# x turned by transfers and one VectorE block transpose instead of by TensorE transposes

## The chip, the cores and the metric

The kernel runs on one core of a Trainium2 chip. TensorE (PE in the profile) multiplies matrices into PSUM; VectorE (DVE), ScalarE (ACT) and GpSimd (POOL) do elementwise work; SyncE (SP) issues the DMAs, all on one queue and in program order. Each engine takes its own instructions in program order and waits for the others through semaphores. The metric is the device time of one execution in microseconds.

## The reference, cut to what matters

x has shape 8 x 2048 x 512: 16384 tokens of 512 features. Two sublayers follow each other. In the attention the axes are named so that, for every token, its 16 heads of 32 numbers attend to each other. The second sublayer routes tokens to experts with a capacity of 8 // 16 = 0, so no expert takes a token, and it comes down to norms:

```python
h = layernorm(x)
Q, K, V = h @ Wq.T + bq, h @ Wk.T + bk, h @ Wv.T + bv     # (8, 2048, 512) -> (8, 16 heads, 2048, 32)
scores = einsum('nqhd,nkhd->nhqk', Q, K) / sqrt(32)       # q, k: heads; h: token
out = einsum('nhql,nlhd->nqhd', softmax(scores), V)       # (8, 16, 2048, 32), read as (8, 2048, 512)
x = x + layernorm(out.reshape(8, 2048, 512) @ Wo.T + bo)
y = layernorm(layernorm(x)) * ln_g + ln_b                 # what is left of the second sublayer
x = x + layernorm(y)
```

All of it is in float32. The products take their left and right operands with the summed index on the partitions, so x, which arrives with tokens on the partitions, has to be turned once so that features lie there.

## The kernel before, in words

The 16384 tokens are 32 units of 512 tokens. A unit is four tiles of 128 tokens; tile t belongs to unit t // 4. Work is written out by hand as strings of two-letter items, and the order of these strings is the program order on every engine at once.

**One tile of x.** `load_x` (L239) brings it into one of four buffers `x`. `stat_x` (L252) takes mean and variance on DVE (L183, L184) and the inverse deviation on POOL (L190, L191). `norm_x` (L257) normalises in place on DVE (L260) and sets the last column to 1 on POOL (L261), because that row of the turned x carries the bias. `turn_x` (L263) makes four 128x128 transposes on TensorE into a PSUM bank `px` (L267), which comes from the same pool of four banks (tag `pj`) as some products. `keep_x` (L270) copies the bank into `xb` on ACT: tiles 0 and 1 of a unit whole (L279), tiles 2 and 3 only their second half (L281). `add_x` (L283) forms four sums of quarters for tiles 2 and 3: two on DVE that read PSUM (L290, L291) and two on POOL (L292, L293). `xb` has seven slots of 2 x 256 columns.

**The products.** Each of q, k and v is a 512x512 by 512x512 product, made with seven products of quarters (`multiply`, L300) instead of eight. Products 1, 6, 7 and 4 of one matrix add up, one on top of the other, in the same PSUM bank ("a"); after each of them `collect` (L323, items `q1e`, `q6e`, ...) copies what the bank then holds on ACT. So 6 can begin only when `1e` has read the bank, 7 only after `6e`, and 4 only after `7e`. Products 5 and 3 share a second bank in the same way: 3 waits for `5e`, which is on DVE. The right operands of products 1 to 7 are slots of `xb`; product 6 needs a sum that POOL makes. The output projection (`d1` to `d7`, `out_multiply` L496 and `out_collect` L512) has the same form: `d6e` and `d7e` are ACT copies at L516, `d5e` is on DVE, and `d6` needs POOL's sums `oS` (`sB`, L476 to L480).

**Steps.** Unit u is worked through in four steps (`step`, L712; strings `STEPS`, L692, and `FIRST_STEPS`, L703, for unit 0). In step c, softmax and weighing of quarter c of unit u run beside the products of unit u+1 (q in steps 0 and 1, k in 1 and 2, v in 2 and 3), the output projection of unit u (d1 in step 3) and of u-1 (the rest in step 0), the final norms of rows of unit u-1 (ra, rv, rg, rf, rt, re, rs), and the reading in of x for unit u+2 (xs, xn, px, xa, xt). The softmax chain of a step is `mx` (DVE maximum and difference, ACT exponential), `dn` (DVE sum and reciprocal, POOL product), `tr` (DVE block transpose, L426), `x0` to `x3` (four ACT copies, L431). Every step ends on TensorE with `sc` (scores, L393) and `av` (weighing, L442); the next step begins with `ok`, the ACT copy of the weighed values, and `mx`.

q, k and v go through DRAM to be spread over partitions: `write` (L356: qs, ks, vs) and `spread_qk`, `spread_v` (L369, L378: qd, kx, vd), four DMAs per matrix and direction. `sk` (kx) is at the head of step 3 and must land before that step's `sc`.

`first_unit` (L597) prepares tiles 0 to 7 and makes the products of unit 0; `last_unit` (L781) ends with the norms of the last rows.

Of the kernel before, what the change touches and what calls it, by code (L numbers as in the profile page):

```python
# [34 lines left out]
F32 = mybir.dt.float32  # L35
BF16 = mybir.dt.bfloat16
AF = mybir.ActivationFunctionType
ALU = mybir.AluOpType
# [12 lines left out]
def head_attention_norms(  # L51
# [15 lines left out]
    nc = tc.nc  # L67
    NB, S, E = x.shape
    P = 128
    H, D = 16, 32  # L70
    assert NB // H == 0, "experts that take tokens"
    EC = E // P
    Q4 = 4
# [7 lines left out]
    xpool = ctx.enter_context(tc.tile_pool(name="xpool", bufs=4))  # L81
    pool2 = ctx.enter_context(tc.tile_pool(name="pool2", bufs=2))
# [24 lines left out]
    oS = const.tile([P, Q4, 2, 2 * P], F32, name="oS")  # L107
    junk = const.tile([P, E], F32, name="junk")
# [130 lines left out]
    def load_x(t):  # L239
        if t < NT:  # L240
            xs[t] = xpool.tile([P, E], F32, tag="x", name=f"x_{t}")
            n, s = divmod(P * t, S)
            nc.sync.dma_start(xs[t], x[n, s : s + P, :] if t < NT - Q4 else renumbered[t % Q4])
# [8 lines left out]
    def stat_x(t):  # L252
        if t < NT:
            mv = moments(xs[t], f"x{t}")
            xrs[t] = mv, rsqrt(mv[:, 1:2], f"x{t}", 1.0, EPS)

    def norm_x(t):  # L257
        if t < NT:
            mv, rs = xrs.pop(t)
            nc.vector.tensor_scalar(xs[t], xs[t], mv[:, 0:1], rs, ALU.subtract, ALU.mult)  # L260
            nc.gpsimd.memset(xs[t][:, E - 1 : E], 1.0)  # L261

    def turn_x(t):  # L263
        if t < NT:
            px[t] = ps_pj.tile([P, EC, P], F32, tag="pj", name=f"px_{t}")
            for ec in range(EC):
                nc.tensor.transpose(px[t][:, ec, :], xs[t][:, ec * P : (ec + 1) * P], ident)  # L267
            del xs[t]

    def keep_x(t):  # L270

        if t < NT:
            u, J = divmod(t, Q4)
            if J == 0:
                xb[u] = pool2.tile([P, 7, 2, 2 * P], F32, tag="xb", name=f"xb_{u}")
            j = slice(P * (J % 2), P * (J % 2) + P)
            if J < 2:
                dst = xb[u][:, 0:2].rearrange("p n e t -> p (n e) t")[:, :, j]
                nc.scalar.copy(dst, px[t])  # L279
            else:  # L280
                nc.scalar.copy(xb[u][:, 2, :, j], px[t][:, 2:4])  # L281

    def add_x(t):  # L283

        if t < NT and t % Q4 >= 2:
            u, J = divmod(t, Q4)
            j = slice(P * (J % 2), P * (J % 2) + P)
            b11, b21, b22, t1, t2, t3, t4 = (xb[u][:, n, :, j] for n in range(7))
            b12 = px[t][:, 0:2]
            nc.vector.tensor_tensor(t3, b22, b12, ALU.subtract)  # L290
            nc.vector.tensor_tensor(t1, b12, b11, ALU.subtract)  # L291
            nc.gpsimd.tensor_tensor(t2, b22, t1, ALU.subtract)  # L292
            nc.gpsimd.tensor_tensor(t4, b21, t2, ALU.subtract)  # L293
# [6 lines left out]
    def multiply(u, name, n):  # L300
        if n == 1:
            banks[name, "a"] = ps_a.tile([P, E], F32, tag="pa", name=f"pa{name}_{u}")
        elif n in (2, 5):
            banks[name, n] = ps_pj.tile([P, E], F32, tag="pj", name=f"p{name}{n}_{u}")
        ps = banks[name, {2: 2, 5: 5, 3: 5}.get(n, "a")]
        w, t = weights[name], sums[name]
        lo, hi = slice(0, 256), slice(256, 512)
        left = {
            1: w[:, 0:2, lo], 2: w[:, 2:4, lo], 3: w[:, 0:2, hi], 4: w[:, 2:4, hi],
            5: t[:, 0], 6: t[:, 1], 7: t[:, 2],  # L310
        }[n]
        right = xb[u][:, {1: 0, 2: 1, 3: 2, 4: 6, 5: 3, 6: 4, 7: 5}[n]]
        if name == "v":
            left, right = right, left
        for m in range(2):
            for e in range(2):
                nc.tensor.matmul(  # L317
                    ps[:, 256 * m : 256 * m + 256],
                    lhsT=left[:, e, P * m : P * m + P], rhs=right[:, e, :],
                    start=(n in (1, 2, 5) and m == 0 and e == 0), stop=(e == 1), skip_group_check=True,  # L320
                )
# [47 lines left out]
    def spread_qk(u, name):  # L369
        if name == "q":  # L370
            qd[u] = pool2.tile([P, H, P], F32, tag="qd", name=f"qd_{u}")
        for J in range(Q4):
            d = slice(32 * J, 32 * J + 32)
            dst = qd[u][d] if name == "q" else kx[d, J % 2]
            src = scratch[name][J // 2, :, J % 2].rearrange("g (d h) t -> d g (h t)", d=D)
            nc.sync.dma_start(dst.rearrange("d (g h) t -> d g (h t)", g=Q4), src)
# [220 lines left out]
    def first_unit():  # L597
# [14 lines left out]
        norm_x(0)  # L612
        turn_x(0)
        keep_x(0)
        stat_x(2)
        norm_x(1)
        turn_x(1)
        keep_x(1)
        stat_x(3)
        norm_x(2)  # L620
        turn_x(2)
        keep_x(2)
        norm_x(3)
        turn_x(3)
        keep_x(3)
# [6 lines left out]
        add_x(2)  # L632
        less_last("q", nc.vector, (1,))
        add_x(3)
# [22 lines left out]
        spread_qk(0, "k")  # L657
        stat_x(6)
        run(0, "v2 v2e v2w v6 v6e")
        turn_x(4)  # L660
        keep_x(4)
        norm_x(6)
        turn_x(5)
# [3 lines left out]
        keep_x(5)  # L667
        load_x(9)
        norm_x(7)
        turn_x(6)  # L670
        keep_x(6)
        load_x(10)
        add_x(6)
        turn_x(7)
        keep_x(7)
        run(0, "v5 v4 v5e v4e v4w v5w")
        stat_x(8)
        add_x(7)
# [4 lines left out]
    def run(u, items):  # L683
# [9 lines left out]
        "lx lr sv st ok sB px mx xa q1 q1e ra d2 ou dn d2e rv d6 d6e tr d5 x0 x1 x2 x3 d7 d7e rg rf q2 rt d5e xs"  # L693
        " d4 q2e re xn d4e d3 d3e rs q2w st sc av",
        "lx lr q6 q6e mx ra dn ok ou q5 rv q7 tr q7e x0 x1 x2 x3 k1 rg rf q5e k1e rt q4 xs q3 q4e re k2 q3e xn"
        " q5w q4w rs px st xa q3w k2e sc av",
        "lx lr k6 k6e mx ra dn ok ou k5 rv k7 tr k7e k2w x0 x1 x2 x3 v1 sq rg k5e rf v1e rt k4 xs k4e k5w k3 re xn"
        " k3e k4w rs px st xa xt k3w sc av",
        "sk lx lr v2 mx v2e ra v6 ok v6e dn ou ds v5 rv sA v7 tr x0 x1 v7e x2 x3 d1 rg rf v5e v2w d1e v4 rt xs"
        " v4e v5w v3 re xn v3e v4w rs px xa xt v3w sc av",  # L700
# [3 lines left out]
        "lx sv mx q1 q1e dn ok ou q2 q2e q6 q6e tr k1 k1e x0 x1 x2 x3 q7 q7e q2w lb xs q5 q5e xn q4 q4e px q5w q4w lo"  # L704
        " xa sc av",
        "lx k2 mx k2e dn ok ou c4 q3 tr k6 k6e x0 x1 x2 x3 q3e k2w q3w k5 xs cs k7 k7e c0 k5e xn px k5w xa sc av",
        "lx mx v1 v1e dn ok ou k4 k4e k3 k3e tr k4w k3w sq c1 v2 x0 x1 x2 x3 v2e xs c2 c3 v6 v6e xn wt px xa xt v2w sc av",
        "sk lx ds v7 v7e mx v5 v5e dn ok ou xs tr v4 v4e xn x0 x1 x2 x3 d1 sA v4w v5w d1e px v3 v3e xa xt v3w lg sc av",
# [3 lines left out]
    def step(u, c):  # L712
# [8 lines left out]
        def keep_last():  # L721
# [9 lines left out]
            "xs": lambda: stat_x(s + 9), "xn": lambda: norm_x(s + 9), "px": lambda: turn_x(s + 8),  # L731
# [3 lines left out]
            "xa": lambda: keep_x(s + 8), "xt": lambda: add_x(s + 8),  # L735
# [142 lines left out]
```

## Time and profile before

| What | Value |
|---|---|
| median of 3 runs | 1885.3 us (1884.98 to 1886.38) |
| span of the profiled execution | 1882.1 us, 3.2 us under that median |
| granted TensorE clock | 0.995 on the mean |
| steps of unit 15 to 16 on TensorE (905.8 to 963.2 us) | 16.0, 14.3, 12.6 and 14.5 us, together 57.4 us |
| busy in these 57.4 us | PE 57.40, DVE 43.93, ACT 36.54, POOL 31.77 us |
| DMA share in the four steps | 0.62, 0.33, 0.80, 0.83 |
| TensorE transposes of x | 512 in the whole, four per tile, 16 per unit |

The rows of the profile name the line, the engine, the operation and the tiles it writes and reads (`px<-ident,x`), with the number in the brackets at the end giving the idle time of the engine before it and what ended it. In the chain a line gives the start, the length and the work that held the end of the kernel back at that time; it is read as "while this stood there, nothing else mattered".

### The profile page before, as it was taken

The page shows a single profiled execution, that of the slowest core. Times are in us where ns is not written, and L with a number is a line of the kernel's source. Part 1 is how long each engine was busy: PE and PEld are TensorE (multiplying, and loading weights), DVE is VectorE, ACT ScalarE, POOL GpSimd, SP SyncE. Part 2 cuts the span into 40 slices and gives each one's busy share as a digit, 9 for nine tenths or more (in the row PEclk, how much of TensorE's full clock was granted, in tenths as well). Part 3 has the DMA queues.
Part 4 walks back from the last instruction along what each step waited for, and adds up shares of the span by engine and source line. Part 5 has one row for each costly group of instructions (what it writes and reads, how often), then busy time and mean ns, then how long its engine had stood idle before and what let it go on. Part 6 is the DMA issues. An engine that isn't in the chain of part 4 may idle for free.

```text
span 1882.1 us, 57927 instructions
## 1 busy us (share of the span) xinstructions
PE 1847.4 (98%) x24026; PEld 1596.9 (85%) x24026; DVE 1423.8 (76%) x2634; ACT 1172.4 (62%) x1910; POOL 1028.9 (55%) x1785
## 2 busy tenths in 40 slices
PE   8999999999999999999999999999999999999994
PEld 7888888888888888888888888888888888888872
DVE  7667777777777777777777777777777777777777
ACT  2556566666666665666666666566666656666666
POOL 5345654555554565555556545555545555455546
PEclk9999999999999999999999999999999999999998
DMA  7765766566766657665667665576556677656671
GB/s 218 187 158 154 186 174 162 152 167 166 181 169 161 166 147 191 175 162 150 171 157 185 172 163 161 154 181 180 161 158 168 157 189 193 165 147 163 154 186 57
DMA packets 370051, 312.58 MB, mean 166 GB/s; under 512 B 149750, under 2 KB 280825, under 8 KB 365564
## 3 DMA queue, kind: packets, MB, share of 16 engines
q1 hardware_dynamic: 369788, 308.89, 63.0%
q8 instruction: 188, 3.08, 0.7%
q14 instruction: 75, 0.61, 0.1%
HBM read 174.59 MB, written 135.27 MB: 165 GB/s over the span
## 4 chain that ended last, share of the span: by engine, by line
PE 93%; POOL 2%; DVE 1%; ACT 1%; DMA 1%; issue 1%; SPq 0%; POOLq 0%; ACTq 0%; DVEq 0%
PE paq L317 12%; PE pak L317 12%; PE pav L317 11%; PE pad L507 11%; PE pk L317 9%; PE pq L317 9%; PE pv L317 9%; PE pd L507 8%; PE sa L393 6%; PE sa L442 4%; PE px L267 3%; ACT ex L431 1%; POOL rs_d L191 1%; POOL e L421 0%; POOL rs_d L190 0%
## 5 line engine op out<-in xcount | busy, mean ns | idle before, releaser
L431 ACT COPY ex<-eT 32x512 f32<-32x512 f32 x512 | 315.5, 616 | 40.1 <-DVE eT L426 31.2
L421 POOL TENSOR_TENSOR e<-e,den 128x512 f32<-128x512 f32 x128 | 134.6, 1052 | 323.2 <-DVE den L420 265.4
L191 POOL TENSOR_TENSOR rs_d<-rs_d,nhalf 128x1 f32<-128x1 f32 x384 | 211.1, 550 | 32.0
L588 POOL TENSOR_TENSOR a<-a,r 128x512 f32<-128x512 f32 x120 | 181.7, 1514 | 44.1 <-ACT a L584 27.0
L190 POOL TENSOR_SCALAR rs_d<-mv_d 128x1 f32<-128x1 f32 x250 | 50.1, 200 | 255.9 <-DVE mv_d L184 242.8
L404 DVE TENSOR_REDUCE top<-sa 128x16 f32<-128x512 f32 x128 | 88.7, 693 | 103.5 <-PE sa L442 66.7
L584 ACT ACTIVATE a<-a,nm,rs_d 128x512 f32<-128x512 f32 x120 | 97.7, 814 | 97.2 <-DVE nm L577 97.2
L414 ACT ACTIVATE e<-e 128x512 f32<-128x512 f32 x128 | 80.8, 631 | 122.7 <-DVE e L406 122.5
L453 ACT COPY oT<-sa 128x512 f32<-128x512 f32 x124 | 134.4, 1084 | 31.8 <-PE sa L442 29.6
L260 DVE TENSOR_SCALAR x<-x,mv_x,rs_x 128x512 f32<-128x512 f32 x128 | 94.7, 740 | 53.5 <-POOL rs_x L191 52.8
L419 DVE TENSOR_REDUCE den<-e 128x16 f32<-128x512 f32 x128 | 87.2, 681 | 62.9 <-ACT e L414 62.8
L393 PEld LDWEIGHTS sa<-kx,qd 64*32 64x32 f32 x8192 | 109.2, 139 | 29.9 <-issue 27.7
L133 ACT COPY sa<-under 128x1024 f32<-128x1024 f32 x129 | 131.7, 1021 | 2.1
L426 DVE STREAM_TRANSPOSE eT<-e 128x512 f32<-128x512 f32 x128 | 91.0, 711 | 54.7 <-POOL e L421 54.7
L393 PE MATMUL sa<-kx,qd 64*32 64x64 f32 x8192 | 129.1, 249 | 1.0 <-DMA vs<-cv 0.9
L543 ACT ACTIVATE junk<-a 128x512 f32<-128x512 f32 x120 | 84.1, 701 | 71.7 <-DVE a L521 71.7
L442 PE MATMUL sa<-ex,vd 64*32 64x64 f32 x8192 | 123.2, 226 | 3.9 <-ACT ex L431 3.4
L317 PE MATMUL paq<-xb,sq 128*128 128x256 f32 x512 | 124.2, 386 | 0.1
L317 PE MATMUL pak<-xb,sk 128*128 128x256 f32 x512 | 124.2, 386 | 0.0
L317 PE MATMUL pv<-wv,xb 128*128 128x256 f32 x512 | 124.1, 385 | 0.0
L317 PE MATMUL paq<-xb,wq 128*128 128x256 f32 x512 | 123.2, 384 | 0.7 <-ACT xb L281 0.4
L317 PE MATMUL pav<-wv,xb 128*128 128x256 f32 x512 | 121.2, 380 | 1.0 <-ACT u3v L337 1.0
(163 smaller groups left out, 4719.8 us busy)
## 6 DMA issues: line engine op xcount, KB each, us to landing
qs<-cq SPq DMA_DIRECT2D x128, 256.0 KB, 2.3
qd<-qs SPq DMA_DIRECT2D x128, 256.0 KB, 5.3
ks<-ck SPq DMA_DIRECT2D x128, 256.0 KB, 2.4
kx<-ks SPq DMA_DIRECT2D x128, 256.0 KB, 4.3
vs<-cv SPq DMA_DIRECT2D x128, 256.0 KB, 3.1
vd<-vs SPq DMA_DIRECT2D x128, 256.0 KB, 4.4
r<-in_x_dram SPq DMA_DIRECT2D x128, 256.0 KB, 4.9
x<-in_x_dram SPq DMA_DIRECT2D x124, 256.0 KB, 4.5
```

The costliest lines, as they stand in the source:

```text
L133: nc.scalar.copy(sa, under.unsqueeze(1).to_broadcast([P, 2, UT]))
L191: nc.gpsimd.tensor_tensor(rs, rs, nhalf, ALU.pow)
L260: nc.vector.tensor_scalar(xs[t], xs[t], mv[:, 0:1], rs, ALU.subtract, ALU.mult)
L317: nc.tensor.matmul(ps[:, 256 * m : 256 * m + 256], lhsT=left[:, e, P * m : P * m + P], rhs=right[:, e, :], start=(n in (1, 2, 5) and m == ...
L393: nc.tensor.matmul(sa[32 * i : 32 * i + 32, t, 64 * rh : 64 * rh + 64], lhsT=qd[u][d].rearrange("p h (b m) -> p (h b) m", b=2)[:, :, m], r ...
L421: nc.gpsimd.tensor_tensor(e, e, den.unsqueeze(2).to_broadcast([P, 16, 32]), ALU.mult)
L431: nc.scalar.copy(ex[q, :, i % 2, :], sm["t"][q])
L442: nc.tensor.matmul(o[:, J], lhsT=vd[u][d, 4 * c + rh, J, :], rhs=ex[d, 8 * (J // 2) + 2 * rh + J % 2].rearrange("p i k -> p (i k)"), start ...
L453: nc.scalar.copy(dst, sa[:, :, 256:].rearrange("p t (k h R) -> p t k h R", k=Q4, h=Q4))
L507: nc.tensor.matmul(ps[:, m], lhsT=left[:, e, P * m : P * m + P], rhs=right[:, e], start=(n in (2, 5) and m == 0 and e == 0), stop=(e == 1) ...
L584: nc.scalar.activation(a, a, AF.Identity, bias=nm, scale=rs)
L588: engine.tensor_tensor(a, a, res.pop((u, k)), ALU.add)
```

## The change

x is no longer turned by TensorE, but for the first four tiles. For every 256 tokens: ACT normalises two tiles into a standing tile `xn` whose last column stays 1; four SBUF-to-SBUF transfers move its four column blocks of 128 onto 32 partitions each (`xm`, into one buffer `xm`); and one DVE block transpose of 128x1024 writes the result straight into `xb` (`px`). For this the rows of a load are interleaved over the partitions and the rows of Wq, Wk and Wv are reordered on the host. The sums read `xb` alone: two on DVE (`xt`) and two on POOL (`xp`), over 128x512 instead of 128x256 and once per unit instead of twice. `xs` now follows `tr` at once in all steps after the first unit's, `xn` comes a little earlier, and in step 0 the products are q1 d2 q2 d6 d5 d7 d4 d3 where they were q1 d2 d6 d5 d7 q2 d4 d3.

```diff
+    xn = const.tile([P, 2, 2, E], F32, name="xn")
...
     def load_x(t):
...
+            src = x[n, s : s + 2 * P, :] if t < NT - Q4 else renumbered[J : J + 2].rearrange("J p e -> (J p) e")
+            nc.sync.dma_start(xs[t], src.rearrange("(b i t) e -> i t b e", b=Q4, i=2)[t % 2])
...
     def norm_x(t):
-            nc.vector.tensor_scalar(xs[t], xs[t], mv[:, 0:1], rs, ALU.subtract, ALU.mult)
-            nc.gpsimd.memset(xs[t][:, E - 1 : E], 1.0)
+            nc.gpsimd.tensor_scalar(nm, mv[:, 0:1], rs, -1.0, ALU.mult, ALU.mult)
+            nc.scalar.activation(
+                normed(t)[:, 0 : E - 1], xs.pop(t)[:, 0 : E - 1], AF.Identity, bias=nm, scale=rs
+            )
...
+    def move_x(h):
+        if h < NT // 2:
+            px[h] = mpool.tile([P, Q4, 2, P], F32, tag="xm", name=f"xm_{h}")
+            for a in range(Q4):
+                src = xn[:, h % 2, :, P * a : P * a + P]
+                nc.sync.dma_start(px[h][32 * a : 32 * a + 32].rearrange("p b i e -> p (b i e)"), src)
+    def turn_x(h):
+        if h < NT // 2:
+            n = 2 * (h % 2)
+            dst = begin_x(h // 2)[:, n : n + 2].rearrange("p n e (c t) -> p (n e) c t", t=32)
+            nc.vector.transpose(dst, px.pop(h).rearrange("p b i (k e) -> p k (b i) e", k=EC))
+    def add_x(u, engine, j=slice(0, 2 * P)):
+            if engine is nc.vector:
+                nc.vector.tensor_tensor(t3, b22, t1, ALU.subtract)
+                nc.vector.tensor_tensor(t1, t1, b11, ALU.subtract)
             else:
+                nc.gpsimd.tensor_tensor(t2, b22, t1, ALU.subtract)
+                nc.gpsimd.tensor_tensor(t4, b21, t2, ALU.subtract)
...
     def first_unit():
         run(0, "k3 k4w k5w k3e k3w")
         spread_qk(0, "k")
+        move_x(2)
         stat_x(6)
         run(0, "v2 v2e v2w v6 v6e")
-        turn_x(4)
-        keep_x(4)
         norm_x(6)
-        turn_x(5)
         stat_x(7)
         load_x(8)
         run(0, "v7 v7e")
-        keep_x(5)
         load_x(9)
         norm_x(7)
-        turn_x(6)
-        keep_x(6)
+        turn_x(2)
         load_x(10)
-        add_x(6)
-        turn_x(7)
-        keep_x(7)
+        move_x(3)
+        stat_x(8)
         run(0, "v5 v4 v5e v4e v4w v5w")
-        stat_x(8)
-        add_x(7)
         run(0, "v3 v3e v3w")
...
     STEPS = (
-        "lx lr sv st ok sB px mx xa q1 q1e ra d2 ou dn d2e rv d6 d6e tr d5 x0 x1 x2 x3 d7 d7e rg rf q2 rt d5e xs"
-        " d4 q2e re xn d4e d3 d3e rs q2w st sc av",
-        "lx lr q6 q6e mx ra dn ok ou q5 rv q7 tr q7e x0 x1 x2 x3 k1 rg rf q5e k1e rt q4 xs q3 q4e re k2 q3e xn"
-        " q5w q4w rs px st xa q3w k2e sc av",
-        "lx lr k6 k6e mx ra dn ok ou k5 rv k7 tr k7e k2w x0 x1 x2 x3 v1 sq rg k5e rf v1e rt k4 xs k4e k5w k3 re xn"
-        " k3e k4w rs px st xa xt k3w sc av",
-        "sk lx lr v2 mx v2e ra v6 ok v6e dn ou ds v5 rv sA v7 tr x0 x1 v7e x2 x3 d1 rg rf v5e v2w d1e v4 rt xs"
-        " v4e v5w v3 re xn v3e v4w rs px xa xt v3w sc av",
+        "lx lr sv st ok sB mx q1 q1e ra d2 ou dn d2e q2 q2e rv d6 d6e xp tr xs d5 x0 x1 x2 x3 d7 d7e rg rf rt d5e "
+        " d4 q2w xn re d4e d3 d3e rs st sc av",
+        "xm lx lr q6 q6e mx ra dn ok ou q5 rv q7 tr xs q7e x0 x1 x2 x3 k1 rg rf q5e k1e rt q4 q3 q4e xn re k2 q3e "
+        " q5w q4w rs st q3w k2e sc av",
+        "lx lr k6 k6e mx ra dn ok ou k5 rv k7 tr xs k7e k2w x0 x1 x2 x3 v1 sq rg k5e rf v1e rt k4 k4e k5w k3 xn re px "
+        " k3e k4w rs st k3w sc av",
+        "sk xm lx lr v2 mx v2e ra v6 ok v6e dn ou ds v5 rv sA v7 tr xs x0 x1 v7e x2 x3 d1 rg rf v5e v2w d1e v4 rt "
+        " v4e v5w v3 xn re v3e px xt v4w rs v3w sc av",
     )
...
     FIRST_STEPS = (
-        "lx sv mx q1 q1e dn ok ou q2 q2e q6 q6e tr k1 k1e x0 x1 x2 x3 q7 q7e q2w lb xs q5 q5e xn q4 q4e px q5w q4w lo"
-        " xa sc av",
+        "lx sv mx q1 q1e dn ok ou px q2 q2e xt xp q6 q6e tr k1 k1e x0 x1 x2 x3 q7 q7e q2w lb xs q5 q5e xn q4 q4e q5w q4w lo"
+        " sc av",
...
-    nc = _bacc.Bacc("TRN2", target_bir_lowering=False, num_devices=1)
+    nc = _bacc.Bacc("TRN2", target_bir_lowering=False, num_devices=1, dynamic_dma_scratch_size=1024)
...
+        if m != "o":
+            w = w.reshape(512, 4, 4, 32).transpose(0, 2, 1, 3).reshape(512, 512)
```

Not shown: the first four tiles still go over TensorE (`norm_first`, `turn_first`, `keep_first`), with the sums from `xb`, and the other three strings of unit 0's steps are changed in the same way as those of the later units (`xm` heads steps 1 and 3, `px` stands late in steps 2 and 3, `xt` late in step 3).

## The prediction

> **What bounds the kernel now.** I read four views, in this order. First the busy times and a stretch of 200 us from the middle:
>
> ```profile
> PE 1847.4 (98%) x24026; PEld 1596.9 (85%) x24026; DVE 1423.8 (76%) x2634; ACT 1172.4 (62%) x1910; POOL 1028.9 (55%) x1785
> ```
>
> ```profile
> 400.00:600.00 200.00, 200.00 (x2631) 174.97 (x2630) 152.99 (x285) 125.57 (x204) 104.93 (x186) 1.00 0.62 163
> ```
>
> TensorE (first pair of numbers after the stretch) is busy 200.00 of 200 us at full clock, DVE 76%, ACT 63%, DMA 62%. Second, the chain of waits from 900 to 960 us, to see what a transpose group costs there:
>
> ```profile
> 903.74 0.44 PE px L267 x4
> 904.18 0.87 PE sa L393 x36
> ...
> 905.78 0.59 PE px L267 x4
> 906.37 1.73 PE paq L317 x8
> ...
> 920.20 0.89 PE sa L393 x50
> 921.10 0.71 PE sa L442 x46
> 921.81 1.92 PE paq L317 x8
> ```
>
> The chain is TensorE end to end, and a tile's four transposes hold it 0.44 us; but those right after `av` (905.78) hide 0.19 us that the next product otherwise pays (1.92 against 1.73). Third, the order in step 0, on TensorE and then on ACT:
>
> ```profile
> 911.40 1.89 PE L507 MATMUL pd<-so,oS 128*128 128x256 f32 x8
> 913.13 1.89 PE L507 MATMUL pad<-so,oS 128*128 128x256 f32 x8
> 914.86 1.89 PE L317 MATMUL pq<-xb,wq 128*128 128x256 f32 x8
> 916.59 1.89 PE L507 MATMUL pad<-wo,oT 128*128 128x256 f32 x8
> ```
>
> ```profile
> 912.54 2.50 ACT L431 COPY ex<-eT 32x512 f32<-32x512 f32 x4 [0.35 <-DVE eT L426]
> 915.07 0.58 ACT L516 COPY a<-pad 128x512 f32<-128x512 f32 x1
> ```
>
> These are d5, d7, q2, d4; the ACT copy at 915.07 is `d7e`. It reads the bank that d4 writes next, and q2's 1.73 us cover it. Fourth, DVE in step 1, and the TensorE row that waits for it:
>
> ```profile
> 928.57 0.75 DVE L566 SCALAR_TENSOR_TENSOR a<-a,rs_d,rb 128x512 f32<-128x512 f32 x1
> 929.24 0.68 DVE L353 TENSOR_TENSOR cq<-pq,u3q 128x512 f32<-128x512 f32 x1
> ```
>
> ```profile
> 930.48 1.89 PE L317 MATMUL pq<-xb,wq 128*128 128x256 f32 x8
> ```
>
> `q5e` ends at 929.92, 0.56 us before q3 (930.48), which may not start earlier. So slack is what the change must live on: TensorE has none to give, the others have, but only in places.
>
> **Part 1: the transposes go.** Tiles 8 to 127, turned in the steps of units 0 to 29: three groups of 0.435 and one of 0.59 - 0.19 = 0.40 per unit make 1.705 us, times 30 is **-51.2 us**. Tiles 4 to 7 come under part 4.
>
> **Part 2: q2 is moved before d6.** Now d7 is followed by d4 at once. d7's last result comes 0.16 us after its issue ends (1.89 against 1.73), `d7e` starts 0.04 later, takes 0.58, and TensorE resumes some 0.04 to 0.1 later: 0.82 to 0.88 us in which TensorE has nothing else, since d3 waits for `d5e`, which needs `d7e` too. I take 0.88, times 30 (steps of units 1 to 30): **+26.4 us**. It holds only if ACT is free. With the end of `av` as zero: q1 takes 1.92, d2, q2, d6, d5, d7 end at 10.57, so `d7e` could start at 10.77. `q2e` and `rv` now stand before `tr` on DVE: q2 is ready at 5.54, `q2e` and `rv` run to 7.0, `tr` 7.0 to 7.7, the four `ex` copies 7.75 to 10.25. That leaves ACT 0.5 us. DVE reaches `q2e` in time if `mx` starts by 2.0 after `av`; in step 3 it now has `px` and `xt` before `mx`. For a 128x1024 transpose no row exists: below, the 0.71 us of 128x512 (L426), above, twice that; rows of 256 and 512 columns (0.41, 0.69) differ by 0.28, so I take 0.71 + 2 x 0.27 = 1.25. An add of 128x512 from SBUF took 0.69 (L168), 1.10 beside a POOL add of 1.05 (L169 at 15.8 us). Starting behind `v3e`, 0.5 before `av` ends, `mx` comes at 1.9 to 2.6, so the copies end at 10.25 to 10.9. Ends: 0.82 and 1.2 us per unit.
>
> The Trainium skill (SBUF — State Buffer, SBUF: two separate sides) speaks against `xt`: it calls the port that DVE shares with POOL an exclusive lock, which a DVE operation with two SBUF inputs takes, and the old form read PSUM. By the rule each `xt` add could lose a whole POOL add, as the first unit's row L169 agrees (2.73 us at 21.9 us beside POOL's 2.69): 2 x 1.27 us (L588) on `mx`, some 2 of them past the slack, would turn the sum from -7.5 to about +52.
>
> The rows of step 0, where DVE's two-SBUF row L552 beside POOL's `oS` adds took 1.03 instead of 0.74 us, keep the adds within my ends.
>
> **Part 3: xs moves ahead of rg and rf in step 1.** Two operations of 0.72 and 0.10 us from start to start delay `q5e` to 930.74; with 0.04 for the signal, q3 loses 0.30 us, times 31: **+9.3 us**. Ends 0.1 (DVE catches up in the 0.46 us that it waits before `tr`) and 0.5 (a restart as dear as after `av`, 0.19). In step 2 `k5e` ends at 943.61 for k3 at 944.89, in step 3 `v5e` at 957.42 for v3 at 959.06: 0.82 fits.
>
> **Part 4: the first units.** Before, v6's copy keeps v7 until 43.87 whether eight transposes lie in between or not, so their 0.87 us are no gain. After it the chain is DMA: SP issues kx until 43.76, then `xm` of tiles 4 and 5, some 0.5 each and 3.4 to landing (between 2.3 for qs and 4.3 for kx): 49.3. DVE turns until 50.6; SP, past v2w and three loads, may issue the second `xm` only then, since `xm` has one buffer: landed about 56. `stat_x(8)` waits on DVE for x_8, loaded 2.4 us later (52), and `v5e` stands behind it, so v3 starts at 53.6, not 50.03. Then sc, mx, dn until 59.3, `px` 60.6, `q2e`, `xt` 62.5, POOL's add 63.8: q6 starts at 63.85, against 56.39. The 0.5 us wait before q4 stays. **+7.5 us**, and 0.5 for 128x512 copies (0.59 for 0.37) and strided norms at the start: **+8**. Ends 4 and 11.
>
> **Part 5: what is covered.** ACT per unit: four norms of 0.81 (L584's form) for copies of 2 x 0.595 and 2 x 0.503, 1.05 us more of 57.4; `xn` stands before `re` on ACT and delays the row norm, POOL's add and the store by 0.8, and SP's `k3w` behind the store by some 0.5. DVE: four norms of 0.74 and four adds of 0.42 (4.64) for two transposes and two adds (about 4.0). POOL: four 0.74 adds and four 0.12 memsets for two 1.27 adds and four 0.30 scalars, nothing. xp lies on POOL before the rsqrt of xs and rt, which have until 12.1. SP issues eight DMAs more per unit; the pair of steps matters, not the count. Step 1's `xm` lands in a quiet time (share 0.33). Step 3's does not:
>
> ```profile
> 950.90 3.19 SPq L376 DMA_DIRECT2D kx<-ks  x4
> ```
>
> ```profile
> 952.00:962.00 10.00, 10.00 (x100) 8.73 (x100) 8.10 (x16) 7.53 (x14) 8.19 (x12) 1.00 1.04 244
> ```
>
> The DMA engines are full (1.04) for 10 us. 512 KB more at 244 GB/s is 2.1 us, behind kx, so kx (landed at 957.9 for `sc` at 961.4) is safe; `xm`, issued from 954.6 to 956.7, lands at about 960.3 (ends 959.0 and 962.0, by the landings of 2.3 for qs and 5.3 for qd). DVE wants it at 961.5: `v3e` ended at 962.2 and comes 0.7 earlier, with a norm and a transpose group before it gone. x, r and vs behind it land 2 us later; vd, landing by 972, is wanted at 979. Cost nothing, with 1.2 us of cover.
>
> **Sum.** -51.2 + 26.4 + 9.3 + 8 = -7.5 us. On the profiled execution (1882.1 span, 3.2 around it, 1885.3, the median itself) that is **1877.8, say 1878 us**. Its own ends: -51.2 + 24.6 + 3 + 4 = -19.6 and -51.2 + 36 + 15.5 + 11 = +11.3; these hardly meet all at once, so 1867 to 1888.
>
> **Rivals.** (a) *No bubbles*: DVE and ACT leave neither d4 nor q3 waiting, or q4-like cover exists that I don't see. Then -51.2 + 8: 1842. For it, no wait of this sort stands in the trace; against it, d4's bank. Chance 0.12. (b) *The transfer of step 3 is late*, slower: DVE waits at `px` with `mx`, `tr` and the `ex` copies behind it, so beyond 0.5 us each us late is a us more before d4, 30 times. From 0.75 us late it eats the 7.5 us; at 1.5 late, 30 us: 1908. For it, the full DMA and 1.2 us of cover that hang on SP's queue; against it, 2.3 us landings of 256 KB (qs). Chance 0.23. (c) *DVE's port*: `xt` beside POOL's add moves `mx` past 2.6, 0.25 us per unit, 7.5 us: 1885, no change. Chance 0.15. My forecast has 0.50.
>
> **How the numbers follow.** 0.2% is 3.8 us, about what a measurement can tell. Of my 0.50, 0.38 is faster, 0.08 same, 0.04 slower; (a) is faster; (c) is 0.04 faster, 0.07 same, 0.04 slower; (b) slower, but for 0.01. So faster 0.54, same 0.16, slower 0.30. The range leaves out (a) and the upper third of (b): 1862 to 1908.
>
> **What would show it.** `px` on TensorE falls to 16 matmuls; step 0 has d4 some 2.6 us after d7's start with ACT's copy in between (part 2); q3 in step 1 waits 0.3 for `cq<-pq,u3q` (part 3); q6 near 64 us (part 4); DVE idle before its 128x1024 transpose, waiting for DMA, would be (b). Wrong it would be made most by a gap before d4 that is far from 0.88, since thirty of them stand against the whole gain.

## The result and the profile after

The changed kernel takes 1951.8 us in the median (1949.56 to 1959.61) against 1885.1 us before (1884.82 to 1886.38): a ratio of 1.036, 95% interval 1.0339 to 1.0381. The forecast was 1878 us, and the time lies above its range (1862 to 1908). One execution of a version below (q2 moved alone) ran at a granted clock of 0.775 and took 2338.5 us; it stands in no median here.

The page's line of busy times after, and the stretch of 200 us that was shown of before (length, then busy time with the number of instructions of PE, PEld, DVE, ACT and POOL, granted clock, DMA share, GB/s):

```profile
PE 1836.2 (94%) x23523; PEld 1545.0 (79%) x23530; DVE 1454.2 (74%) x2510; ACT 1200.0 (61%) x1910; POOL 1088.0 (56%) x1723
```

```profile
400.00:600.00 200.00, 191.56 (x2419) 162.83 (x2418) 151.68 (x263) 123.99 (x197) 115.09 (x180) 0.98 0.76 180
```

The transposes are gone from TensorE (some 500 matmuls fewer), but it now stands still for 8.4 us of these 200. The chain of waits around the step boundary of unit 15, where before it was TensorE end to end, now runs through the transfer and VectorE:

```profile
943.24 5.90 DMA xm<-xn
...
949.26 1.26 DVE xb L315
950.52 0.02 issue
950.54 0.70 DVE xb L322
951.24 0.02 issue
951.26 0.69 DVE xb L323
951.96 0.61 DVE top L437
```

`av` ends and q1 starts at 948.50; call that T0. The transfer `xm` lands at 949.14, `px` (L315) starts at T0+0.76 and the two adds of `xt` (L322, L323) follow. Only then comes `top`, the first operation of `mx`, at T0+3.37. Before, in the same unit, it began 1.3 us after the end of `av` (905.7), 0.80 us after q1, which one tile's transposes kept back:

```profile
907.00 0.69 DVE L404 TENSOR_REDUCE top<-sa 128x16 f32<-128x512 f32 x1 [1.22 <-ACT oT L453]
```

What this does to the end of step 0, on TensorE (d5, d7, d4, d3) and on ACT (the `ex` copies and `d7e`):

```profile
955.54 1.89 PE L540 MATMUL pd<-so,oS 128*128 128x256 f32 x8
957.26 1.89 PE L540 MATMUL pad<-so,oS 128*128 128x256 f32 x8
960.70 1.99 PE L540 MATMUL pad<-wo,oT 128*128 128x256 f32 x8 [1.55 <-ACT a L549]
962.86 1.99 PE L540 MATMUL pd<-wo,oS 128*128 128x256 f32 x8 [0.17 <-DVE a L554]
```

```profile
957.54 2.50 ACT L464 COPY ex<-eT 32x512 f32<-32x512 f32 x4 [1.22 <-DVE eT L459]
960.07 0.59 ACT L549 COPY a<-pad 128x512 f32<-128x512 f32 x1
```

ACT waits 1.22 us for the softmax, so its copies end at T0+11.5 and `d7e` runs at 960.07. From d7 to d4, now its successor, it takes 3.44 us; before, d7 and the q2 behind it took 1.73 each. d3 is late too, because `rg` and `rf` ahead of `d5e` on DVE run beside POOL's two `xp` adds:

```profile
958.22 1.39 DVE L595 SCALAR_TENSOR_TENSOR a<-r,mv_d,rg 128x512 f32<-128x512 f32 x1
959.71 1.57 DVE L599 SCALAR_TENSOR_TENSOR a<-a,rs_d,rb 128x512 f32<-128x512 f32 x1
```

```profile
957.79 1.27 POOL L325 TENSOR_TENSOR xb<-xb 128x512 f32<-128x512 f32 x1
959.14 1.59 POOL L326 TENSOR_TENSOR xb<-xb 128x512 f32<-128x512 f32 x1
```

Before, the same two took 0.71 and 0.75 there:

```profile
912.43 0.71 DVE L562 SCALAR_TENSOR_TENSOR a<-r,mv_d,rg 128x512 f32<-128x512 f32 x1
913.25 0.75 DVE L566 SCALAR_TENSOR_TENSOR a<-a,rs_d,rb 128x512 f32<-128x512 f32 x1
```

In step 1, DVE's `q5e` (first fence) makes q3 start 2.03 us after q4 instead of 1.73 (second fence), as the prediction said:

```profile
974.71 0.68 DVE L386 TENSOR_TENSOR cq<-pq,u3q 128x512 f32<-128x512 f32 x1
```

```profile
973.41 1.89 PE L350 MATMUL paq<-xb,wq 128*128 128x256 f32 x8
975.44 1.99 PE L350 MATMUL pq<-xb,wq 128*128 128x256 f32 x8
```

Where the time of units 2 to 29 went, from the distances between the first matmuls of successive products (28 units, profiled executions; SA stands for what `sc` and `av` put on TensorE at the end of a step):

| Place | us in all |
|---|---|
| transposes gone, 28 x 1.705 | -47.7 |
| d7 to d4, 3.53 on the mean for 1.73 | +50.3 |
| d4 to d3 and d3 to SA (2.27 for 1.73, 1.93 for 1.82) | +18.4 |
| step 1: q4 to q3 2.03 for 1.73, q3 to k2 1.83 for 1.73 | +11.2 |
| stops inside SA at the ends of steps 2 and 3 | +15.5 |
| q1, d2, q2 of step 0: half clock in the units after such a stop, and three more stops, in d2 | +13.1 |
| sum; measured 1664.0 - 1603.0 | +60.8; +61.0 |

Ahead of unit 2 the start costs 12.5 us (unit 2 begins at 173.60 for 161.12), unit 30 and what follows 2.3: together 75.8, the difference of the two spans (1957.8 and 1882.1). The profiled execution of after took 1959.6 us, 8 us above the median of 1951.8, so what varies, the stops above all, may be somewhat large here.

A unit made of the median distances takes 58.2 us instead of 57.2 (the median of whole units, which has stops in it, is 58.6). The forecast had 56.7.

### The profile page after: what moved, and what is told of

It reads as the page before. It is cut to its first block, busy times and chain, and to the rows that moved or that the text cites. A ratio compares the mean times of both kernels' runs of the same rounds, so it can differ in the third digit from the quotient of the medians.

```text
span 1957.8 us, 57123 instructions
## 1 busy us (share of the span) xinstructions
PE 1836.2 (94%) x23523; PEld 1545.0 (79%) x23530; DVE 1454.2 (74%) x2510; ACT 1200.0 (61%) x1910; POOL 1088.0 (56%) x1723
## 4 chain that ended last, share of the span: by engine, by line
PE 36%; DVE 27%; DMA 14%; issue 6%; POOL 6%; ACT 5%; SPq 5%; DVEq 0%; POOLq 0%; ACTq 0%
DMA xm<-xn 7%; PE pk L350 5%; PE pak L350 5%; PE paq L350 5%; PE pq L350 4%; PE pd L540 4%; PE sa L426 4%; DMA ks<-ck 3%; DVE a L599 3%; PE pav L350 3%; PE sa L475 3%; SPq L308 3%; DVE den L452 2%; POOL e L454 2%; PE pv L350 2%
## 5 line engine op out<-in xcount | busy, mean ns | idle before, releaser
L464 ACT COPY ex<-eT 32x512 f32<-32x512 f32 x512 | 315.8, 617 | 62.6 <-DVE eT L459 53.6
L621 POOL TENSOR_TENSOR a<-a,r 128x512 f32<-128x512 f32 x120 | 156.5, 1304 | 196.6 <-ACT a L617 196.6
L193 POOL TENSOR_TENSOR rs_d<-rs_d,nhalf 128x1 f32<-128x1 f32 x384 | 220.6, 574 | 31.9
L284 ACT ACTIVATE xn<-x,nmx,rs_x 128x511 f32<-128x511 f32 x124 | 105.8, 853 | 202.8 <-POOL nmx L283 183.3
L540 PE MATMUL pad<-wo,oT 128*128 128x256 f32 x480 | 122.0, 399 | 49.0 <-ACT a L549 49.0
L540 PEld LDWEIGHTS pad<-wo,oT 128*128 128x128 f32 x480 | 92.1, 197 | 73.1 <-ACT a L549 61.0
L486 ACT COPY oT<-sa 128x512 f32<-128x512 f32 x124 | 134.3, 1083 | 12.5 <-PE sa L475 10.3
L350 PE MATMUL paq<-xb,wq 128*128 128x256 f32 x512 | 130.8, 400 | 0.9 <-DVE wq L157 0.6
L350 PE MATMUL pq<-xb,wq 128*128 128x256 f32 x512 | 126.1, 390 | 4.1
L599 DVE SCALAR_TENSOR_TENSOR a<-a,rs_d,rb 128x512 f32<-128x512 f32 x120 | 122.7, 1023 | 9.3
```

Source lines behind the costliest of these rows:

```text
L193: nc.gpsimd.tensor_tensor(rs, rs, nhalf, ALU.pow)
L350: nc.tensor.matmul(ps[:, 256 * m : 256 * m + 256], lhsT=left[:, e, P * m : P * m + P], rhs=right[:, e, :], start=(n in (1, 2, 5) and m == ...
L464: nc.scalar.copy(ex[q, :, i % 2, :], sm["t"][q])
L486: nc.scalar.copy(dst, sa[:, :, 256:].rearrange("p t (k h R) -> p t k h R", k=Q4, h=Q4))
L540: nc.tensor.matmul(ps[:, m], lhsT=left[:, e, P * m : P * m + P], rhs=right[:, e], start=(n in (2, 5) and m == 0 and e == 0), stop=(e == 1) ...
L599: nc.vector.scalar_tensor_tensor(a, a, rs, row_const["b"], ALU.mult, ALU.add)
```

## The experiments

The first theory (A in the texts below) was the prediction's rival (b): the transfer of step 3 lands late. Against it stood the order of step 0 alone, the traffic of the transfers, and the port that VectorE shares with GpSimd.

### Without transfers, and with transfers nobody waits for

```diff
-            nc.vector.transpose(dst, px.pop(h).rearrange("p b i (k e) -> p k (b i) e", k=EC))
+            nc.vector.transpose(dst, xn[:, h % 2].rearrange("p i (b k e) -> p k (i b) e", b=Q4, k=EC))
```

In the first run the four transfers of `move_x` are left out as well.

> The changed kernel with the SBUF-to-SBUF transfers left out: the VectorE block transpose reads the normed x itself, so what reaches the products is x in a wrong order of tokens; every other instruction stays. Theory A (the second transfer of a unit lands late and holds the transpose px at the end of step 3): the distance from d7 to d4, 3.45 us in the median of the changed kernel, falls to the 2.56 of its best units, 0.89 x 28 = 25 us, so about 1927; if the stalls on `issue` and the half-clock stretches (34 us over units 2 to 29) come from the same transfers' traffic, they go too, and 1893 is reached. Theory B (transfers harmless, the loss is the order of step 0 and the shared port): 1945 or more.

> The changed kernel with its transfers kept, but the block transpose reads the normed x instead of what they write, so nothing waits for them (x reaches the products in a wrong order of tokens). Theory A, by the wait: like the run without transfers in the distance d7 to d4 (2.56), about 1927. Theory C (the traffic itself, by full DMA engines, starves the fetch of instructions and stretches the loads and stores): the 34 us of irregular units stay here and go only where the transfers are left out, so 1927 here against 1893 there. Theory B: 1945 or more in both.

Measured: 1925.4 us without transfers (1922.94 to 1926.61), 1943.0 us with transfers that nobody waits for (1939.69 to 1944.79). The first number is what theory A gave, and yet theory A is refuted by the trace: from d7 to d4 still takes 3.44 us in the median unit without any transfer (3.43 in the other run). What was won lies elsewhere: the start, the stops, and the units in which the transfer had landed very late. A total that fits says nothing about the place. VectorE of the run without transfers, T0 = 926.16, and GpSimd beside it:

```profile
925.55 1.23 DVE L313 STREAM_TRANSPOSE xb<-xn 128x1024 f32<-128x1024 f32 x1
926.82 1.73 DVE L320 TENSOR_TENSOR xb<-xb 128x512 f32<-128x512 f32 x1
928.57 0.69 DVE L321 TENSOR_TENSOR xb<-xb 128x512 f32<-128x512 f32 x1
929.18 0.68 DVE L435 TENSOR_REDUCE top<-sa 128x16 f32<-128x512 f32 x1
```

```profile
926.72 1.27 POOL L619 TENSOR_TENSOR a<-a,r 128x512 f32<-128x512 f32 x1 [1.64 <-ACT a L615]
```

`px` is now on time, T0-0.61, where the prediction wanted it. But GpSimd's last add to the rows starts 0.10 us ahead of `xt`, and the first `xt` add takes 1.73 us instead of 0.69. So `top` comes at T0+3.02, hardly earlier than with the late transfer. One limit had hidden the other.

### The port: one GpSimd add less

```diff
     def rows_last(u, k, engine=nc.gpsimd):
-        engine.tensor_tensor(a, a, res.pop((u, k)), ALU.add)
+        r = res.pop((u, k))
+        if k != 2:
+            engine.tensor_tensor(a, a, r, ALU.add)
```

> The changed kernel without its transfers (as the run without transfers, 1925.4) and without one add of GpSimd: the last addition to the rows in step 3 (one of four per unit, a<-a,r), so those rows of the output lack a term. Theory P (shared port): in the run without transfers px starts on time, 0.61 us ahead of T0, the start of step 0's q1, but the first of the two VectorE adds behind it takes 1.72 us beside that GpSimd add, not 0.69, so the softmax's first reduction begins at T0+3.0; without the add it begins at about T0+2.0, d7 to d4 falls from 3.44 to 2.56, 0.87 x 25 units = 22 us, 1903. Theory Q (the VectorE queue is too long by px and both adds, port or not): d7 to d4 stays over 3.3, 1920 or more.

> The changed kernel with its transfers, without the same GpSimd add in step 3 (those rows of the output lack a term). Theory D (two limits, one behind the other: with transfers px starts at T0+0.76, after the GpSimd add, so the port costs nothing there; without them the port takes over): no gain in the typical unit, 1945 or more. Theory P alone: 22 us less, 1930.

> The changed kernel with its transfers running but not waited for (as in the run of 1943.0) and without GpSimd's last add to the rows in step 3 (x in a wrong order of tokens, those rows lack a term). With it the four cases stand beside one another at the same traffic: wait and add 1951.8, wait alone 1955.5, add alone 1943.0, neither: this one. Theory D (two limits, one behind the other): only with both gone does d7 to d4 fall to 2.56, 22 to 25 us off 1943, about 1920. Theory Q (queue too long in any case): 1938 or more.

Measured: 1900.4 us without add and transfers (1899.09 to 1902.7), 1955.5 with transfers and wait (1953.15 to 1956.48), 1919.2 with transfers that nobody waits for (1912.01 to 1921.25). Medians over units 2 to 29, relative to T0:

| Run | `px` starts | first `xt` add | `top` starts | d7 to d4 | time |
|---|---|---|---|---|---|
| before, from the end of `av` | | | 1.28 | 3.46 (q2 between) | 1884.6 |
| after: wait and add | 0.66 | 0.69 | 3.27 | 3.45 | 1951.8 |
| wait, no add | 0.62 | 0.69 | 3.65 | 3.52 | 1955.5 |
| add, no wait | -0.61 | 1.71 | 3.00 | 3.43 | 1943.0 |
| neither | -0.60 | 0.69 | 2.09 | 2.56 | 1919.2 |
| no transfers, add | -0.59 | 1.71 | 3.02 | 3.44 | 1925.4 |
| no transfers, no add | -0.61 | 0.69 | 2.09 | 2.56 | 1900.4 |

Theory D (two limits, one behind the other) is shown: with either limit alone d7 to d4 stays at 3.4 to 3.5, and only with both gone does it fall to 2.56. Unit by unit it follows `top`: in the 196 units of after, the five runs above and the run with xs and xp put back (below), d7 to d4 is 2.56 or 2.57 wherever `top` starts by T0+2.14, 2.68 at T0+2.24, and 3.3 or more from T0+2.88 on, unless d7 itself was held up. Taking away the GpSimd add is worth 23.8 us where `px` is on time (1943.0 to 1919.2) and nothing where it is late. That the run with wait and no add is no faster at all has a row too: with the row add gone GpSimd does its `oS` adds earlier, and the second `xt` add runs beside one of them, 1.10 us in the median instead of 0.69. The waits of TensorE for `d7e` tell the same in two lines, after and then the run with neither:

```profile
PE pad L540 <- ACT a L549: 49.0, 30, 2.8
```

```profile
PE pad L541 <- ACT a L550: 20.3, 30, 0.7
```

The 20.3 us that remain (0.68 each) are the move of q2.

### The order of step 0

q2 moved alone, in the kernel before:

```diff
-d2e rv d6 d6e tr d5 x0 x1 x2 x3 d7 d7e rg rf q2 rt d5e xs d4 q2e re
+d2e q2 q2e rv d6 d6e tr d5 x0 x1 x2 x3 d7 d7e rg rf rt d5e xs d4 re
```

> The kernel before with one part of the change alone: q2 and its copy moved ahead of d6 in step 0. The prediction's term: 0.88 us per unit between d7 and d4, 30 units, +26 us, 1911; the best units of the changed kernel show 0.83, +25. If order were harmless: 1885. If it were worth all that the changed kernel shows between d7 and d4 (1.72): +52, 1937.

> The kernel before with q2 and its copy ahead of d6 once more (1912.6 in its first runs), for its trace: the whole +28.5 should stand between d7 and d4, 2.56 to 2.75 us instead of 3.46 for d7, q2 and d4 together less q2's 1.73, with every other distance as before. If part of it stands elsewhere (start, d2 to d6), the prediction's term was right by accident.

Measured: 1912.6 us, and 1911.7 us in the second set of runs; 27 to 28 us over before. TensorE and ACT of the second:

```profile
870.80 1.89 PE L507 MATMUL pad<-so,oS 128*128 128x256 f32 x8
873.37 1.99 PE L507 MATMUL pad<-wo,oT 128*128 128x256 f32 x8 [0.68 <-ACT a L516]
875.20 1.89 PE L507 MATMUL pd<-wo,oS 128*128 128x256 f32 x8
```

```profile
869.75 2.50 ACT L431 COPY ex<-eT 32x512 f32<-32x512 f32 x4
872.73 0.58 ACT L516 COPY a<-pad 128x512 f32<-128x512 f32 x1 [0.47 <-PE pad L507]
```

ACT waits for d7 and not d7's copy for ACT: 2.56 us from d7 to d4 in every unit, and 0.10 for the restart in d4 to d3 (1.83). That is 0.93 x 30 = 28 us of the 29.0 by which the two spans differ (1911.1 and 1882.1). In units 2 to 29 the other places are as before, but for 0.9 us less at d6; another 1.7 us stand in the start. Then q2 back in the changed kernel:

```diff
-d2e q2 q2e rv d6 d6e xp tr xs d5 x0 x1 x2 x3 d7 d7e rg rf rt d5e d4 q2w xn re d4e d3 d3e rs
+d2e rv d6 d6e xp tr xs d5 x0 x1 x2 x3 d7 d7e rg rf q2 rt d5e d4 q2e xn re d4e d3 d3e rs q2w
```

> The changed kernel with q2 of step 0 put back between d7 and d4 (the order of before, transfers and all else as changed). With d4 late by 1.72 us in the median unit and q2 1.73 us long, q2 covers the whole of it: d7 to q2 1.73, q2 to d4 1.8, so 1.72 x 28 = 48 us less, about 1904, whatever makes d7's copy late. If instead the wait only moves on (px late, then d4's successor d3 or the next product late by as much), 1940 or more.

Measured: 1929.7 us (1925.96 to 1937.07): less than half of what was expected came. d7 to q2 is 1.73 again, but d6 now takes 2.80 us in the median from its start to that of d5, with the wait in the middle of it:

```profile
941.26 0.59 PE L540 MATMUL pad<-so,oS 128*128 128x256 f32 x2
942.69 1.56 PE L540 MATMUL pad<-so,oS 128*128 128x256 f32 x6 [0.84 <-POOL oS L510]
```

d6 reads `oS`, which GpSimd adds from ACT's `oT` copy, and both come late at this boundary. q2 ahead of d6 had covered that; behind d7 it covers `d7e`. One product cannot cover both, so the boundary itself has to be cleared.

### xs of step 1 and xp put back

```diff
-d6 d6e xp tr xs d5 ... d4 q2w xn re d4e          (step 0)
+d6 d6e tr xs d5 ... d4 q2w xn xp re d4e
-rv q7 tr xs q7e ... rt q4 q3 q4e xn              (step 1)
+rv q7 tr q7e ... rt q4 xs q3 q4e xn
```

> The changed kernel with two moves undone that are read at different places of the trace: the statistics of x (xs) in step 1 put back behind q4, and in step 0 GpSimd's two adds (xp) put behind the next norm, away from the row gain and shift (rg, rf). xs: q4 to q3 from 2.03 to 1.73 and q3 to its successor from 1.83 to 1.73, 0.40 x 30 = 12 us. xp: rg and rf fall from 1.39 and 1.57 to 0.72 and 0.75, so d4 to d3 from 2.17 to 1.73 and d3 to SA from 1.92 to 1.82, 0.54 x 28 = 15 us. Both: 1925. If what is freed only moves on to the next wait: 1945 or more.

Measured: 1932.7 us (1928.53 to 1936.65), 19 us less; 27 were expected. Both mechanisms are where they were said to be: q4 to q3 and q3 to k2 are 1.73 again in every unit, d4 to d3 is 1.83 and d3 to SA 1.82 in the median; `rg` falls from 878 to 719 ns and `rf` from 1023 to 825 on the mean. The estimate missed that some units keep a longer d4 to d3 for the half clock (below), and d7 to d4 stays at 3.46.

### A version with the boundary cleared

x is normed one tile earlier, the transfers start at the heads of steps 1 and 2, `px` stands late in steps 1 and 2, `xt` in VectorE's idle time of step 3, `xp` behind the norm of step 0, q2 and xs as before; unit 1 is turned on TensorE as before.

```diff
-if t < Q4:                 (load_x)
+if t < 2 * Q4:
-"xn": lambda: norm_x(s + 9), "xm": lambda: move_x(s // 2 + 4),
+"xn": lambda: norm_x(s + 10), "xm": lambda: move_x(2 * u + 3 + c),
-"px": lambda: turn_x(2 * u + 3 if s == 0 else 2 * u + 4 + (c == 3)),
+"px": lambda: turn_x(2 * u + 3 + c),
+step 0: ... d7 d7e rg rf q2 rt d5e xs d4 q2e xn xp re d4e d3 d3e rs q2w st sc av
+step 1: lx lr xm q6 q6e ... rt q4 xs q3 q4e xn re k2 px q3e ...
+step 2: lx lr xm k6 k6e ... rt k4 xs k4e k5w k3 xn re px k3e ...
+step 3: ... d1e v4 rt xs v4e v5w v3 xt xn re v3e v4w rs v3w sc av
```

> A version that keeps the transfers for units 2 and later and clears the step boundary: x is normed one tile earlier, the transfers start at the heads of steps 1 and 2, the block transposes stand late in steps 1 and 2, VectorE's adds in its idle time of step 3, GpSimd's adds behind the norm in step 0; q2 and xs stand where before has them; unit 1 is turned on TensorE as before. If the losses of the changed kernel are what the traces say (mx, the softmax's head, late by px and the adds; port; xs; start): units of 55.5, 1885 - 29 x 1.705 = 1836, and up to 18 more for the transfers' traffic (1943.0 against 1925.4): 1836 to 1854. If moving them only moves the wait: 1885 or more.

Measured: 1883.0 us (1878.8 to 1886.6), ratio to before 0.9988 (0.9979 to 0.9997): no better than before. The unit takes 56.9, not 55.5. The loss had moved: from the start of d2 to that of d6 it took 2.19, and from d6 to d5 2.69, with the wait inside d2 and inside d6 (the expectation of the next version names the pairs one place earlier). ACT of that run around T0 = 902.69:

```profile
902.15 0.81 ACT L284 ACTIVATE xn<-x,nmx,rs_x 128x511 f32<-128x511 f32 x1 [2.11 <-POOL nmx L283]
902.87 0.80 ACT L618 ACTIVATE a<-a,nm,rs_d 128x512 f32<-128x512 f32 x1
...
904.19 1.06 ACT L487 COPY oT<-sa 128x512 f32<-128x512 f32 x1
```

The new norm on ACT waits 2.11 us for GpSimd, with the rows' norm and the copy `oT` queued behind it, and d2 and d6 need `oT`. So the norm of that tile was moved into step 0, and the rows' norm of step 3 ahead of `xt`:

```diff
-step 3: ... v3 xt xn re v3e          step 0: ... d4 q2e xn xp re d4e
+step 3: ... v3 re xt v3e             step 0: ... d4 q2e yn xn xp re d4e     (yn: the norm of tile s + 9)
```

> The version with early transfers, with one thing mended. Its units took 56.9 us, not 55.5: in step 3 ScalarE's norm of x waits for GpSimd (nmx, done only at T0-0.6), and the copy oT of the scores behind it begins at T0+1.5, so d2 and d6 wait (q1 to d2 2.19, d2 to d6 2.69). Here that norm is moved into step 0 behind d4, and the rows' norm of step 3 ahead of VectorE's two adds. If the norm's place was the cause: q1 to d2 and d2 to d6 back at 1.73, 1.4 us x 28 = 39 us off 1883, about 1844. If ScalarE or VectorE is full and the wait moves on: 1870 or more.

Measured: 1848.2 us (1844.65 to 1852.99), ratio 0.9804 (0.9787 to 0.982): faster than both kernels. The chain of waits is TensorE again, every product 1.73 or, behind `av`, 1.92:

```profile
845.77 0.90 PE sa L427 x51
846.66 0.71 PE sa L476 x50
847.38 1.92 PE paq L351 x8
849.30 1.73 PE pq L351 x8
851.03 1.73 PE paq L351 x8
```

The median unit is 55.51 us, 1.71 less than before: the whole of the transposes. Units 2 to 29 together gain 36.1 us of 47.7 in the profiled execution; 9.8 of the rest stand in SA.

```diff
+            px[h] = None          (the last version, move_x without its four transfers)
```

> The last version (1848.2) without its SBUF-to-SBUF transfers (x reaches the products in a wrong order of tokens): what the transfers' traffic still costs where nothing waits for them. In the changed kernel the same step, from transfers that nobody waits for to none, was worth 1943.0 - 1925.4 = 17.6 us, in the start and in stops of TensorE inside SA that last 3.4 us instead of 6.1. If it is the traffic: 1831 to 1840. If those stops have nothing to do with it: 1846 or more.

Measured: 1843.4 us (1840.68 to 1845.77). That lies between the two expectations, and its interval (0.9761 to 0.9797) overlaps that of the version with transfers: the traffic costs some 5 us here, if anything, and the extra time in SA stays (8.7 us for 9.4, of which 3.0 are waits for kx). In the changed kernel the same step was worth 17.6 us, of which 7.5 lay ahead of unit 2.

## Why the prediction was wrong

**The transposes (-51.2): right.** The last version's unit is shorter by 1.71 us, the 1.705 of the working.

**q2 moved (+26.4): right for what it priced, wrong by its condition.** Alone in the kernel before, the move cost 27 to 28 us, 0.83 between d7 and d4 and 0.10 behind. But the term was taken on the condition that "DVE reaches `q2e` in time if `mx` starts by 2.0 after `av`". The condition was nearly exact: up to `top` at 2.14, d7 to d4 is 2.56. It did not hold: `top` came at 3.27 in the median, and d7 to d4 cost 50.3 us over units 2 to 29.

**What is covered ("Cost nothing, with 1.2 us of cover"): the step that failed.** The transfer of step 3 was put, by bandwidth, at an issue from T0-7.4 to T0-5.3 and a landing at T0-1.7. In unit 15 it was issued from T0-7.3 to T0-4.6 (0.67 us per issue, not 0.5) and landed at T0+0.64, 5.3 us after the last issue and not 3.6; it stood behind kx, and the DMA share from 942 to 950 was 1.15. So rival (b) is what happened, at a chance of 0.23. Its price was nearly right: `px` is 1.16 us late in the median (T0+0.66 for T0-0.5), which by its formula gives 0.66 us per unit; measured were 0.89. What it did not have is the units in which the landing was later still (d7 to d4 4.2 to 4.8 us) and in some of which TensorE then ran at half clock (d4 to d3 3.3 to 3.4).

**The port: the second half of the same step.** The prediction bounded an `xt` add by 0.69 alone and 1.10 beside a GpSimd add of 1.05 us. Beside the row add of 1.27 us it took 1.71. Rival (c) was to give 0.25 us per unit; where the transfer is not in the way it gives 0.87, 23.8 us. The working had weighed a rule of the Trainium skill (SBUF — State Buffer, SBUF: two separate sides): an operation of VectorE with two SBUF inputs waits until a GpSimd operation that holds the shared port has ended. The row agrees with it: 926.82 to 928.55 is the rest of the GpSimd add, to 927.99, and 0.56 of its own. The rule gave about +52 for the sum, nearer to the +66.7 measured than the -7.5 of the rows chosen. That is luck in part: one of the two adds met a GpSimd add, not both, so 1.02 us were lost and not 2 x 1.27, and much of the +66.7 stands elsewhere. Both estimates treated lateness and port as separate; they are two limits of nearly equal size on one queue, of which only the later one counts.

**What was not in the sum: `xp` beside `rg` and `rf`.** The prediction looked at `xp` only for GpSimd's own due times ("xp lies on POOL before the rsqrt of xs and rt"), not for what it does to VectorE. It cost 0.44 in d4 to d3 and 0.10 behind, and the run that moved it away shows it.

**xs in step 1 (+9.3): mechanism right, size 0.40 instead of 0.30.** The delay of q3 was 0.30 as worked out; the restart behind it cost another 0.10. (The strings that were changed so run in 30 units, 1 to 30; the prediction counted 31.)

**The start (+8): the waits right, the half clock missing.** Unit 2 begins 12.5 us late, where +8 with the other terms of units 0 and 1 makes 5.8. v3 began at 53.75 us (53.6 expected, 50.03 before) and q6 at 65.98 (63.85 expected, 56.39 before). Behind the waits of 4.06 and 3.94 us, for DVE and for `xp`, both products ran at half clock: 3.65 and 3.78 us for 1.89, at a granted clock of 0.53 and 0.50.

**Stops: not in the sum at all.** 15.5 us inside SA and 13.1 in and around d2 in the profiled execution; they end when TensorE's instructions arrive (last section).

The miss between the two profiled executions (spans of 1957.8 and 1882.1: +75.7 us where -7.5 had been said, so 83.2), term by term:

| Term | us beyond the forecast |
|---|---|
| d7 to d4: 50.3 for 0.88 x 28 = 24.6 | 25.7 |
| d4 to d3 and d3 to SA, `xp` | 18.4 |
| xs: 11.2 for 0.30 x 28 = 8.4 | 2.8 |
| stops in SA, and q1, d2, q2 | 28.6 |
| ahead of unit 2: 12.5 for 5.8 | 6.7 |
| unit 30 and the end: 2.3 for 1.2 | 1.1 |
| sum; measured | 83.3; 83.2 |

The first line is explained by the runs. With xs and xp put back, 19 us of some 27 in the second and third came back as time. What the stops of the fourth wait for the kept traces show, not why they come where they do. The first alone would have turned a gain of 7.5 into a loss of 18.

## What to carry to other kernels

Work that is taken from the engine that bounds the kernel has to be placed, not only hidden by its share of busy time: an in-order queue that is 74% busy can still have its work just ahead of the one operation everybody waits for. Price such a step at the boundary by when its last input lands and by what the other engine on the shared port does at that moment, and count both as a maximum, since removing one then shows nothing. And when an experiment gives the expected total, look whether the time went from the expected place: the run without transfers gave theory A's number, and from d7 to d4 nothing had changed. Last, a change that takes instructions from an engine also moves the places in the program at which its next instructions have to be there.

## What the runs showed of the hardware

**Half clock after a short stop.** Of the changed kernel's TensorE rows, two d4 with their d3, after stops of almost the same length:

```profile
780.56 3.52 PE L540 MATMUL pad<-wo,oT 128*128 128x256 f32 x8 [2.54 <-ACT a L549]
783.87 2.10 PE L540 MATMUL pd<-wo,oS 128*128 128x256 f32 x8
```

```profile
1314.64 1.99 PE L540 MATMUL pad<-wo,oT 128*128 128x256 f32 x8 [2.49 <-ACT a L549]
1316.81 1.99 PE L540 MATMUL pd<-wo,oS 128*128 128x256 f32 x8 [0.18 <-DVE a L554]
```

The windows of the same kernel behind these two stops, granted clock before the last two numbers:

```profile
780.50:783.90 3.40, 3.34 (x9) 2.69 (x10) 2.26 (x5) 0.62 (x2) 2.15 (x6) 0.55 0.17 50
```

```profile
1314.60:1318.00 3.40, 3.18 (x14) 2.50 (x15) 2.85 (x6) 0.63 (x1) 2.14 (x6) 1.00 0.20 61
```

After 2.54 us of standing still eight matmuls took 3.52 us at a granted clock of 0.55; after 2.49 us, 1.99 us at 1.00. So the stop of 2.54 us cost 1.53 us beyond itself, and 0.11 on d3. No sharp limit comes out of the traces. In the thirteen profiled executions at full speed, between 100 and 1760 us, the granted clock fell to one half, for 3.41 us or twice that, during or within 2.2 us behind 2 of 253 stops of TensorE of 0.3 to 1.5 us, 6 of 88 of 1.5 to 2 us (the shortest 1.72), 17 of 40 of 2 to 3 us and 13 of 14 longer ones. The Trainium skill (TensorE: Matmul & The Clock Gate, 🎯 Why this matters for your kernels) warns of idle gaps of more than about 3 us; here 2.54 was enough in after, and 1.72 in the first version with the boundary cleared.

**Stops that end when instructions arrive.** Every nine units (in after at the end of step 3 of units 3, 12 and 21 and of step 2 of units 1, 10, 19 and 28; in the last version at the end of step 3 of units 8, 17 and 26) TensorE stands still in the middle of `av` while the rows show no wait, and then goes on; in after it does so in d2 as well (units 9, 18, 27). The first two lines are of after, the third of the last version:

```profile
PE sa L475 <- issue: 14.4, 7, 3.9
PE pd L540 <- issue: 4.5, 3, 2.8
```

```profile
PE sa L476 <- issue: 5.1, 3, 2.3
```

Neither before nor its version with q2 moved has any such stop in the steady units; all versions with the turn off TensorE have them, with transfers and without. So neither the transfers' traffic nor the order of q2 makes them. The kept traces show what ends them. Beside the queue of the kernel's own transfers the page of after lists a queue of instructions:

```profile
q8 instruction: 185, 3.03, 0.6%
```

Its 185 packets have 16 KB each, and the trace has 47302 instructions of TensorE (47053 of them matmuls and weight loads), 255.7 per packet; before it is 188 packets and 48303 instructions, 256.9 per packet. Number these instructions in order of their start. In units 2 to 29 of the eleven versions with the turn off TensorE there are 66 such stops of over 0.6 us. All 66 come before an instruction whose number leaves 193 when divided by 256, and all end 1.2 to 1.5 us after a packet of this queue has ended. So TensorE waits there for its own instructions, at the same place between one packet's share and the next. Before, and with q2 moved, each packet had ended at least 2.0 us ahead of the instruction at that place. An SA has 256 matmuls and weight loads in 1.6 us, as many as a packet holds, and nine units of after have 13312 instructions, 52 x 256, so the same products meet that place again every nine units. Without the 32 instructions that a unit's transposes took, the places fall elsewhere than before. In the changed kernel the transfers make the stops longer: at the end of step 3 of units 3, 12 and 21 they last 3.9, 3.5 and 3.3 us in after and 1.5, 1.4 and 1.5 us without the transfers. Why a packet starts so late at some of these places, and not before the change, no run shows.
